# Attention sums turned and multiplied with Wo one slot later, in a two-part kernel on one core

## The chip, the core and the metric

The kernel runs on one core of a Trainium2 chip. The time is the device time of one launch in microseconds: 4896.63 us as the median of three runs (4894.68 to 4904.67). The engines named below are PE (TensorE: matrix products and transposes; its weight loads are listed apart as PEld), DVE (VectorE), ACT (ScalarE), POOL (GpSimd) and SP (SyncE, which issues the transfers). All data is float32.

## The reference

The input x is 8 sequences of 512 tokens of 128 features. Two parts follow one another, each behind a layer norm and with its input added to its output:

```python
x = x + attn(layernorm(x), Wqkv, Wo)     # 16 heads of 8, causal; weights 1/(lam - s),
                                         # lam by 4 Newton steps, then normalized
x = x + stack(layernorm(x), ...)         # 6 layers:
for i in range(6):
    x = attn_layer(shift_tokens(x), Wqkv[i], q_scale[i], k_scale[i], Wo[i]) + x
    x = ffn_layer(shift_tokens(x), ln_g[i], ln_b[i], W1[i], b1[i], W2[i], b2[i]) + x
```

attn_layer has 16 heads of 64, normalizes and rotates queries and keys, and lets each window of 32 tokens see itself and the window before. The softmax weights multiply the values, the sum is divided by the sum of the weights, and the heads' outputs are multiplied with Wo (1024 to 128). ffn_layer is a layer norm, a product to 2 x 341 features, a gated Gelu and a product back to 128. shift_tokens moves half of the features one token on.

## The kernel before

The first part is a generator, `stieltjes`, that yields four times in each of its four Newton steps (16 yields, `STEPS`, to a batch of four heads). Sequence 1 runs beside sequence 0 in a stage of its own before the second part begins. The other sequences of the first part are then advanced a few steps per slot of the second part, until `goal` reaches their total some 150 slots before the end. What the second part needs is forced earlier by `need`, which calls `enter` (a fetch of `x2`, a layer norm and four transposes into `xT[b]`). Reads of x and x2 go through `fetch`, into the tile `xb`: for the projection of a sequence, for its end (`sequence_end`, which adds the result to x and writes `x2`), and for `enter` (the last layer's own read of x2 into `xr` aside).

The second part is one loop over slots, t. A unit is a pair of layer and sequence (48 units). The sequences go in groups, (0, 1), then (2, 3, 4), then (5, 6, 7), and within a group the layers are the outer order, so a sequence's next layer comes two units later in the first group and three units later in the others. A unit has four quarters of two pairs of heads, so eight pairs and eight slots. In slot t the code has, in this order:

- `turn(a)`: queries and keys of pair t are transposed (L665) and copied by ACT (L670).
- `gather(last)`: for pair t - 3, 64 small products of weights and values (L719) into the PSUM tile `po2`; DVE takes the reciprocal of the weights' sums (L727) and multiplies (L728) into the SBUF tile `o2`, here called `o`.
- `turn_weights(done)`: the weights of pair t - 2 are transposed (L708) and copied by ACT (L709).
- `prepare_qk`: half of the queries and keys of a coming quarter. Two products (L599, each in two matmuls) and, for each, a square on ACT (L605), the rotation on DVE (L608), a sum on DVE (L614) and an addition on POOL (L616), and at the end the scaling on POOL (L627).
- `exponentials` of pair t - 1 on ACT (L701), and `gelus`.
- `turn_sums(last)`: `o` is transposed (L736, four transposes) and copied by ACT into `oT` (L740).
- `weigh(a)`: 64 small products for the scores of pair t (L684) into the PSUM tile `s2`, then the mask on DVE (L689), the maximum (L694) and the subtraction on POOL (L695).
- `prepare_v`: the values of the coming quarter (L636, ACT copy L639), and every other slot `spread`, 18 transfers of values on SP's queue, and in some slots the loads of the next layer's weights.
- some pieces of the feed-forwards that wait in `parts`.
- `leave(last)`: `oT` times Wo (L744), summed in the PSUM tile `acc` over a unit's eight pairs. After the eighth, DVE adds `acc` to `xT[b]` (L924) and the feed-forward is put into `parts`.

The feed-forward is a generator with seven pieces (eight in the last layer): shift (POOL, L567 to L569); transposes, copy and statistics (L765, L767, L771, L772); normalization (L775 to L778); transposes and ACT's scaling (L785, L787); the product for the gates and its bias (L793, L796); Gelu and the second product and its multiplication with the gates (L754, L804, L807); the product back and the addition to `xT[b]` (L814, L817). One piece is run in each slot, but four in each slot in which the pair that leaves belongs to the first group. There the same sequence's next layer is opened (`open_quarter`, whose shift reads `xT[b]`) three slots after the slot of L924, so a unit's feed-forward must have been traced by then.

PSUM is divided among four pools: two banks for the first part, three with the tag "mm" that rotate among the second part's tiles, one pair of banks with the tag "two" and a single buffer, which `po2` and `s2` use in turn, and one bank for `acc`:

```python
both = ps_b.tile([P, 2, N], F32, name="s2", tag="two")     # weigh
po = ps_b.tile([P, 2, N], F32, name="po2", tag="two")      # gather
```

The order of the code is a priority, not the order of issue: the framework orders each engine's instructions at build time by readiness in an estimate of its own, and puts in the waits. What an engine has been given it runs in that order.

Of the kernel before, what the change touches and what calls it, by code (L numbers as in the profile page):

```python
# [9 lines left out]
F32 = mybir.dt.float32  # L10
# [6 lines left out]
P = 128  # L17
N = 512
NT = N // P
D = 128  # L20
# [9 lines left out]
DHL = 64  # L30
# [20 lines left out]
def tile_kernel(  # L51
# [36 lines left out]
    groups_of = ((0, 1), (2, 3, 4), (5, 6, 7)) if NB == 8 else (tuple(range(NB)),)  # L88
    units = [(l, b) for grp in groups_of for l in range(DEPTH) for b in grp]
# [5 lines left out]
    pj = ctx.enter_context(tc.tile_pool(name="pj", bufs=1))  # L95
# [71 lines left out]
    def streams(pools, bank1):  # L167

        ns_p, dp, tr, pj, sm = pools

        def fetch(src):
            xb = pj.tile([P, NT, D], F32, name="xb", bufs=2)
            nc.sync.dma_start(xb, src.rearrange("(c p) d -> p c d", p=P))
            return xb

# [333 lines left out]
    tp = ctx.enter_context(tc.tile_pool(name="tp", bufs=1))  # L509
# [36 lines left out]
    def load_wo(l, hv):  # L546
        wo = wp.tile([P, NPAIR // 2, D], F32, name="wo", tag=f"wo{hv}")
        nc.sync.dma_start(wo, f_wo[l][hv * HC : (hv + 1) * HC, :].rearrange("(c p) d -> p c d", p=P))
        return wo

    def load_tables(l, h):
        tab = wp.tile([P, 2, 4, DHL], F32, name="tab", tag=f"tab{h}")
        nc.sync.dma_start(tab, tabs[l][:, 2 * h : 2 * h + 2])
        return tab
# [19 lines left out]
    def bank(shape, name):  # L574
        if done_steps >= (4 * NB + 1) * STEPS:
            turns["n"] += 1
            if turns["n"] % 5 > 2:
                return ps_1.tile(shape, F32, name=name, tag="p1")
        return ps_a.tile(shape, F32, name=name, tag="mm")

    PQ = 2
# [77 lines left out]
    def turn(a):  # L659
        g, p = a["g"], a["p"]  # L660
        a["qT"] = qT = []
        for t in range(2):
            pt = bank([P, N], "ptq")
            for c in range(NT):
                nc.tensor.transpose(  # L665
                    pt[:, c * P : (c + 1) * P],
                    g["qn"][:, c, t, 2 * p : 2 * p + 2, :].rearrange("p h e -> p (h e)"), ident,
                )
            q = tp.tile([P, N], F32, name=f"qT{t}")
            nc.scalar.copy(q, pt)  # L670
            qT.append(q)
# [27 lines left out]
    def exponentials(a):  # L699
        flat = a["pr"].rearrange("p c e k -> p (c e k)")  # L700
        follow(nc.scalar.activation(flat, flat, AF.Exp), marks["act"])  # L701

    def turn_weights(a):
        pr = a["pr"]
        a["prT"] = prT = tp.tile([P, NT, P], F32, name="prT")
        pT = bank([P, NT, P], "pT2")
        for c in range(NT):
            nc.tensor.transpose(pT[:, c, :], pr[:, c].rearrange("p e k -> p (e k)"), ident)  # L708
        nc.scalar.copy(prT, pT)  # L709

    def gather(a):
        g, p, prT = a["g"], a["p"], a["prT"]
        po = ps_b.tile([P, 2, N], F32, name="po2", tag="two")
        po = po[:, :, 0 : NT * (DHL + 1)].rearrange("p e (c f) -> p e c f", c=NT)
        for n in range(NQ):
            c, u = n // UB, n % UB
            for e in range(2):
                rows = slice(e * KB, (e + 1) * KB)
                nc.tensor.matmul(  # L719
                    po[u * QB : (u + 1) * QB, e, c, :],  # L720
                    lhsT=prT[rows, c, u * QB : (u + 1) * QB],
                    rhs=g["v3"][rows, n, p, :],
                    start=True, stop=True,
                )
        a["o"] = o = tp.tile([P, NT, 2, DHL], F32, name="o2")
        rs = tp.tile([P, 2, NT], F32, name="rs", bufs=2)
        nc.vector.reciprocal(rs, po[:, :, :, DHL])  # L727
        nc.vector.tensor_tensor(  # L728
            o.rearrange("p c e f -> p e c f"), po[:, :, :, 0:DHL],
            rs.unsqueeze(3).to_broadcast([P, 2, NT, DHL]), ALU.mult,  # L730
        )

    def turn_sums(a):
        pt = bank([P, N], "po3")
        for c in range(NT):
            nc.tensor.transpose(  # L736
                pt[:, c * P : (c + 1) * P], a["o"][:, c].rearrange("p e f -> p (e f)"), ident
            )
        a["oT"] = oT = tp.tile([P, N], F32, name="oT2")
        nc.scalar.copy(oT, pt)  # L740

    def leave(a, wo, acc):
        pp = a["g"]["qt"] * PQ + a["p"]
        nc.tensor.matmul(  # L744
            acc, lhsT=wo[:, pp % (NPAIR // 2), :], rhs=a["oT"],
            start=(pp == 0), stop=(pp == NPAIR - 1),
        )
# [3 lines left out]
    def gelus():  # L751
        if waiting:
            flat = waiting.pop().rearrange("p k n -> p (k n)")
            g = follow(nc.scalar.activation(flat, flat, AF.Gelu), marks["act"])  # L754
            marks["act"] = follow(
                nc.scalar.preload_act_table_set("natural_log_exp_and_others"), g
            )
# [74 lines left out]
    LAG = 2  # L832
# [4 lines left out]
    wo = {hv: load_wo(l0, hv) for hv in range(2)}  # L837
# [5 lines left out]
    def need(b):  # L843
        if b not in entered:
            advance(ready_at.get(b, 0))
            enter(b)
            entered.add(b)

    def open_quarter(i):
        u, qt = quarters[i]  # L850
        groups.append(begin(u, qt, shifted(units[u][1], ep) if qt == 0 else groups[-1]["xs"]))

    def prepared(g):
        u, qt = g["u"], g["qt"]
        spread(g)
        if u + 1 < len(units) and units[u + 1][0] != units[u][0]:
            if qt % 2:
                wq[qt // 2] = load_qkv(units[u + 1][0], qt // 2)
# [8 lines left out]
    pairs, parts, acc = [], [], None  # L867
    slots = len(quarters) * PQ
    t = -1
    while t < slots + LAG + 1 or parts:  # L870
        i, p = t // PQ, t % PQ
        a = done = last = ahead = None
        if 0 <= i < len(quarters):
            a = dict(g=groups[i], p=p)
            pairs.append(a)
        if LAG <= t < len(pairs) + LAG:
            done = pairs[t - LAG]
        if LAG + 1 <= t < len(pairs) + LAG + 1:
            last = pairs[t - LAG - 1]
        if a:  # L880
            turn(a)
        if last:
            gather(last)
        if done:
            turn_weights(done)

        i, h = (t + 1) // PQ + 1, (t + 1) % PQ
        if i < len(quarters):
            if h == 0:
                open_quarter(i)  # L890
            ahead = groups[i]
            cs = (2 * h, 2 * h + 1)
            prepare_qk(ahead, wq[ahead["qt"] // 2], tab[h], cs)
            u = ahead["u"] + 1
            if ahead["qt"] == NS // PQ - 1 and u < len(units) and units[u][0] != units[u - 1][0]:
                tab[h] = load_tables(units[u][0], h)
        if 1 <= t < len(pairs) + (0 if a else 1):
            exponentials(pairs[t - 1])
        gelus()
        if last:  # L900
            turn_sums(last)
        if a:
            weigh(a)
        if ahead:
            prepare_v(ahead, wq[ahead["qt"] // 2], cs)
            if h == PQ - 1:
                prepared(ahead)
        many = 1
        if last and len(parts) + 1 and units[last["g"]["u"]][1] in groups_of[0] and len(groups_of) > 1:
            many = 4  # L910
        for _ in range(many):
            parts = [n for n in parts if next(n, n) is not n]
        if last:
            u, qt = last["g"]["u"], last["g"]["qt"]
            l, b = units[u]
            hv = qt // 2
            if last["p"] == 0 and qt == 0:
                acc = ps_c.tile([P, N], F32, name="acc")
            leave(last, wo[hv], acc)
            if last["p"] == PQ - 1:  # L920
                if qt % 2 and u + 1 < len(units) and units[u + 1][0] != l:
                    wo[hv] = load_wo(units[u + 1][0], hv)
                if qt == NS // PQ - 1:
                    nc.vector.tensor_tensor(xT[b], xT[b], acc, ALU.add)  # L924
                    parts.append(feed_forward(u, *w12[0]))
        t += 1
        u = (t + 6) // NS
        if u < len(units):
            need(units[u][1])
        lead = 3 * NS * DEPTH  # L930
        goal = 5 * STEPS + (total - 5 * STEPS) * (t + 1) // (slots - lead - NS)
        advance(min(goal, total))
# [51 lines left out]
```

## Time and profile before

| | |
|---|---|
| median of three runs | 4896.63 us |
| the profiled execution's own time | 4896.56 us |
| its span | 4894.9 us |
| PE busy | 4172.2 us, 85% |
| DVE busy | 4155.8 us, 85% |
| ACT busy | 3517.7 us, 72% |
| POOL busy | 2990.9 us, 61% |
| L740, ACT's copy of the turned sums | 384 of 585 ns, 283.8 us idle before them |
| L744, the products with Wo | 768 of 606 ns |
| L728, the division on DVE | 384 of 684 ns |

A line of a group gives the source line, the engine, the operation, what it writes and reads, the count, the busy time and the mean of one, and after the bar the idle time of that engine just before these instructions with the work that ended it. A line of a wait gives the total, the times and the longest, in microseconds. Idle time of an engine that is not the bottleneck costs nothing. The first part ends near 3520 us, and it is thin from about 3430 us on; after that the second part is alone.

### The profile page before, as it was taken

The numbers are of one execution on the slowest core, as the hardware profiler recorded it, in microseconds if no ns is written. First come the engines' busy times: TensorE is split into PE (matmuls) and PEld (weight loads), VectorE is DVE, ScalarE is ACT, GpSimd is POOL, SyncE is SP. The second block draws the span as 40 slices with busy tenths as digits, with TensorE's granted clock in tenths as the row PEclk, the third lists the DMA queues.
The fourth block names the chain that finished last, engine by engine and source line by source line (L and its number), as shares of the span: only waits on it lengthen the run. The fifth ranks groups of instructions, "written<-read, shape, count | busy, mean of one in ns | idle before, by whom it ended". The sixth has DMA issues, their size and how long they took to land. (4 is left out here: it accounts for less than half of the span.)

```text
span 4894.9 us, 165932 instructions
## 1 busy us (share of the span) xinstructions
PE 4172.2 (85%) x68749; PEld 2525.4 (52%) x68749; DVE 4155.8 (85%) x9460; ACT 3517.7 (72%) x6298; POOL 2990.9 (61%) x3822
## 2 busy tenths in 40 slices
PE   4555788888888888898888888888999999999998
PEld 1232455544555454554555555555566666666664
DVE  8787888988999989988889999898787777777775
ACT  6898777777777777766777777777566666666664
POOL 3543666656566655666666665666566666666763
PEclk7666899999999999999999999999999999999999
DMA  1000222222222222222222222222233333333332
GB/s 47 1 1 26 52 65 52 62 59 54 59 54 69 61 56 46 65 59 46 63 53 57 53 48 67 47 55 59 65 89 79 80 87 71 85 73 83 85 72 57
DMA packets 558914, 288.89 MB, mean 59 GB/s; under 512 B 97580, under 2 KB 541264, under 8 KB 558160
## 3 DMA queue, kind: packets, MB, share of 16 engines
q1 hardware_dynamic: 558160, 278.26, 24.4%
q8 instruction: 543, 8.90, 0.8%
q14 instruction: 211, 1.73, 0.1%
HBM read 66.21 MB, written 7.34 MB: 15 GB/s over the span
## 5 line engine op out<-in xcount | busy, mean ns | idle before, releaser
L616 POOL TENSOR_TENSOR qn<-qr 128x512 f32<-128x512 f32 x768 | 979.1, 1275 | 1157.1 <-DVE qr L608 1128.4
L608 DVE TENSOR_TENSOR qr<-m,tab 128x1024 f32<-128x1024 f32 x768 | 935.6, 1218 | 293.8 <-ACT sq L605 245.9
L627 POOL TENSOR_TENSOR qn<-qn,ss 128x512 f32<-128x512 f32 x768 | 785.5, 1043 | 113.5 <-ACT ss L624 91.4
L599 PE MATMUL m<-wqkv,xs 128*128 128x512 f32 x1536 | 767.4, 616 | 54.9 <-ACT qT L670 43.8
L281 ACT ACTIVATE d<-ns,lam 128x416 f32<-128x416 f32 (+7 forms) x1024 | 577.8, 623 | 138.4 <-DVE lam L299 103.2
L605 ACT ACTIVATE sq<-m 128x512 f32<-128x512 f32 x768 | 459.1, 598 | 261.9 <-DVE ss L614 180.6
L264 POOL TENSOR_TENSOR df<-ns,lam 128x160 f32<-128x160 f32 (+7 forms) x1024 | 400.6, 427 | 330.5 <-DVE lam L299 207.7
L284 DVE BATCH_NORM_STATS2 stw<-d 128x6 f32<-128x416 f32 (+7 forms) x1024 | 520.5, 561 | 95.7 <-ACT d L282 94.5
L670 ACT COPY qT<-ptq 128x512 f32<-128x512 f32 x768 | 426.4, 586 | 167.2 <-PE ptq L665 165.2
L614 DVE TENSOR_REDUCE ss<-sq 128x8 f32<-128x512 f32 x768 | 517.5, 674 | 0.0
L636 PE MATMUL pv<-wqkv,xs 128*128 128x256 f32 x1536 | 450.1, 416 | 58.4 <-DVE qr L608 43.7
L665 PEld LDWEIGHTS ptq<-ident,qn 128*128 128x128 f32 x3072 | 356.1, 143 | 255.7 <-issue 91.4
L665 PE MATMUL ptq<-ident,qn 128*128 128x128 f32 x3072 | 454.6, 282 | 38.7 <-ACT v L639 22.1
L695 POOL TENSOR_TENSOR pr<-pr,nm 128x512 f32<-128x512 f32 x384 | 400.2, 1042 | 68.7 <-DVE nm L694 57.0
L316 PE MATMUL dTp<-ident,ns 128*128 128x128 f32 x1280 | 245.4, 314 | 224.1 <-ACT ns L304 134.2
L740 ACT COPY oT<-po 128x512 f32<-128x512 f32 x384 | 224.5, 585 | 283.8 <-PE po L736 283.5
L252 PE MATMUL s<-kn,qj 32*32 32x224 f32 (+15 forms) x4096 | 365.7, 430 | 71.3 <-DVE mn L256 59.0
L744 PE MATMUL acc<-oT,wo 128*128 128x512 f32 x768 | 402.2, 606 | 2.7 <-ACT oT L740 2.7
L719 PE MATMUL po<-v,prT 64*32 64x65 f32 x24576 | 393.7, 226 | 6.8 <-DVE pr L689 6.6
L599 PEld LDWEIGHTS m<-wqkv,xs 128*128 128x128 f32 x1536 | 265.4, 197 | 255.2 <-issue 121.3
L282 ACT ACTIVATE d<-d 128x1856 f32<-128x1856 f32 (+1 forms) x256 | 393.0, 1535 | 0.0
L719 PEld LDWEIGHTS po<-v,prT 64*32 64x32 f32 x24576 | 289.8, 106 | 167.4 <-issue 107.2
(135 smaller groups left out, 8118.3 us busy)
## 6 DMA issues: line engine op xcount, KB each, us to landing
v<-v SPq DMA_DIRECT2D x2304, 65.0 KB
v<-v SPq DMA_DIRECT2D x768, 48.8 KB
wqkv<-in_L_ffn_Wqkv_dram SPq DMA_DIRECT2D x72, 256.0 KB
v<-v SPq DMA_DIRECT2D x384, 32.5 KB
wqkv<-in_L_ffn_Wqkv_dram SPq DMA_DIRECT2D x72, 128.0 KB
wo<-in_L_ffn_Wo_dram SPq DMA_DIRECT2D x36, 256.0 KB
tab<-tabs SPq DMA_DIRECT2D x36, 256.0 KB
w<-in_L_ffn_W_dram SPq DMA_DIRECT2D x18, 341.0 KB
```

What stands on the lines that cost most here:

```text
L281: nc.scalar.activation(o, n, AF.Ln, bias=lam[:, c : c + 1])
L284: nc.vector.bn_stats(t["st"][:, 4 * rb + a].rearrange("p u k -> p (u k)"), o)
L599: nc.tensor.matmul(m.rearrange("p t h e -> p t (h e)"), lhsT=xs[:, c * P : (c + 1) * P], rhs=wqkv[:, 0:2, q0 : q0 + HQ * DHL], start=True, ...
L605: marks["act"] = nc.scalar.activation(sq, m.rearrange("p t h e -> p (t h) e"), AF.Square)
L608: nc.vector.tensor_tensor(qr, m.unsqueeze(1).to_broadcast([P, 2, 2, HQ, DHL]), tab[:, i].rearrange("p (k t) e -> p k t e", k=2).unsqueeze( ...
L614: nc.vector.tensor_reduce(ss[:, i, :], sq, axis=AX.X, op=ALU.add)
L616: nc.gpsimd.tensor_tensor(g["qn"][:, c].rearrange("p t h (u e) -> p (t h) u e", u=2), halves_of[:, 0], halves_of[:, 1, :, ::-1, :], ALU.add,)
L627: nc.gpsimd.tensor_tensor(qc, qc, ss[:, i, :].unsqueeze(2).to_broadcast([P, 2 * HQ, DHL]), ALU.mult)
L636: nc.tensor.matmul(pv[:, i], lhsT=xs[:, c * P : (c + 1) * P], rhs=cols, start=True, stop=True,)
L665: nc.tensor.transpose(pt[:, c * P : (c + 1) * P], g["qn"][:, c, t, 2 * p : 2 * p + 2, :].rearrange("p h e -> p (h e)"), ident,)
L670: nc.scalar.copy(q, pt)
L719: nc.tensor.matmul(po[u * QB : (u + 1) * QB, e, c, :], lhsT=prT[rows, c, u * QB : (u + 1) * QB], rhs=g["v3"][rows, n, p, :], start=True, s ...
```

## The change

The pair whose sums are turned, copied and multiplied with Wo is no longer the pair that is gathered in the same slot (`last`, t - 3) but the one gathered a slot before (`gone`, t - 4). The tile `o2` gets a second buffer, and `xb` gives one of its two up. The loop runs one slot more. Everything that hangs on the product with Wo comes a slot later: the addition to `xT[b]`, the reload of Wo and the start of the feed-forward. In the first group the feed-forward's pieces per slot go from four to nine, so that all of them are traced in the slot after it is put into `parts`.

```diff
         def fetch(src):
-            xb = pj.tile([P, NT, D], F32, name="xb", bufs=2)
+            xb = pj.tile([P, NT, D], F32, name="xb")
...
-        a["o"] = o = tp.tile([P, NT, 2, DHL], F32, name="o2")
+        a["o"] = o = tp.tile([P, NT, 2, DHL], F32, name="o2", bufs=2)
...
-    while t < slots + LAG + 1 or parts:
+    while t < slots + LAG + 2 or parts:
...
+        if LAG + 2 <= t < len(pairs) + LAG + 2:
+            gone = pairs[t - LAG - 2]
...
-        if last:
-            turn_sums(last)
+        if gone:
+            turn_sums(gone)
...
-        if last and len(parts) + 1 and units[last["g"]["u"]][1] in groups_of[0] and len(groups_of) > 1:
-            many = 4
+        if gone and len(parts) + 1 and units[gone["g"]["u"]][1] in groups_of[0] and len(groups_of) > 1:
+            many = 9
         for _ in range(many):
             parts = [n for n in parts if next(n, n) is not n]
-        if last:
-            u, qt = last["g"]["u"], last["g"]["qt"]
+        if gone:
+            u, qt = gone["g"]["u"], gone["g"]["qt"]
             l, b = units[u]
             hv = qt // 2
-            if last["p"] == 0 and qt == 0:
+            if gone["p"] == 0 and qt == 0:
                 acc = ps_c.tile([P, N], F32, name="acc")
-            leave(last, wo[hv], acc)
-            if last["p"] == PQ - 1:
+            leave(gone, wo[hv], acc)
+            if gone["p"] == PQ - 1:
```

More of the change, by code (lines that the diff above doesn't have):

```diff
@@ L869, in tile_kernel @@
     t = -1
-    while t < slots + LAG + 1 or parts:
+    while t < slots + LAG + 2 or parts:
         i, p = t // PQ, t % PQ
-        a = done = last = ahead = None
+        a = done = last = gone = ahead = None
         if 0 <= i < len(quarters):
```

## The prediction

> **What bounds the kernel now.** I read the page first (shares of the span in 40 slices), then three long stretches of the span, the groups of instructions by line, the waits stretch by stretch, and the timeline around one ordinary slot and one unit boundary. The slices first:
>
> ```profile
> span 4894.9 us, 165932 instructions
> ...
> PE   4555788888888888898888888888999999999998
> ...
> DVE  8787888988999989988889999898787777777775
> ```
>
> There are four stages. Up to about 555 us the first part runs alone. Then both parts run together until about 3430 us, and from there the second part alone. In the stretches below the columns are length, then busy time of PE, PE's weight load, DVE, ACT and POOL:
>
> ```profile
> 555.00:1790.00 1235.00, 1068.53 (x17300) 632.78 (x17277) 1108.02 (x2589) 917.95 (x1644) 763.66 (x994) 0.96 0.25 59
> 1790.00:3430.00 1640.00, 1416.43 (x23038) 845.30 (x23038) 1469.27 (x3430) 1244.08 (x2225) 1032.08 (x1352) 0.96 0.24 55
> 3430.00:4895.00 1465.00, 1396.80 (x25730) 896.00 (x25730) 1135.07 (x1916) 906.02 (x1772) 944.99 (x929) 0.99 0.34 77
> ```
>
> The reader is to see that the first two have DVE at 90% and PE at 86%, neither full, and that the last one is PE's, at 95% with its drain and 97% without (389.15 of 400 us between 3800 and 4200). So a PE wait that goes in the last stage is worth its full length, and one that goes in the first two only part of it. The two groups that the change is about, the turning of the divided sums (L736) and the scores of the next pair (L684), with idle time and its releasers at the end of the line:
>
> ```profile
> L736 PE MATMUL po<-ident,o 128*128 128x128 f32 x1536 | 244.1, 281 | 82.9 <-DVE o L728 50.9 <-ACT prT L709 20.0 <-DVE sw L294 3.8
> L684 PE MATMUL s<-qT,qT 64*32 64x64 f32 x24576 | 348.8, 227 | 6.7 <-DVE o L728 4.5 <-DVE lam L270 1.3 <-ACT qT L670 0.9
> ```
>
> PE stands 50.9 us in all before the turning, because the division on DVE (L728) is late. The scores hardly wait for it, but only because they come right behind the turning: the sums (`po2`) and the scores (`s2`) share one PSUM tile with the tag "two" and one buffer, so L684 too may not start before L728 has read `po2`. An ordinary slot of the last stage shows the order:
>
> ```profile
> 4199.93 0.69 DVE L728 TENSOR_TENSOR o<-po,rs 128x512 f32<-128x512 f32 x1
> 4199.99 1.88 PE L599 MATMUL m<-wqkv,xs 128*128 128x512 f32 x4
> ...
> 4201.71 0.60 PE L736 MATMUL po<-ident,o 128*128 128x128 f32 x4
> ...
> 4202.24 0.86 PE L684 MATMUL s<-qT,qT 64*32 64x64 f32 x64
> ```
>
> Here the division ends at 4200.62, under the four projections, and PE runs without a gap. The turning takes 0.53 us of PE (4201.71 to 4202.24). The waits by stretch (total, times, longest), first for 600 to 1800 us, then 1800 to 3400, then 3450 to 4840:
>
> ```profile
> PE pn L785 <- DVE xt L778: 20.1, 10, 5.1
> ...
> PE po L736 <- DVE o L728: 8.8, 10, 2.6
> ```
> ```profile
> PE po L736 <- DVE o L728: 24.4, 14, 4.1
> ```
> ```profile
> PE po L736 <- DVE o L728: 11.4, 22, 3.2
> ```
>
> The remaining 6.3 us, six times, lie in the drain and between these stretches.
>
> **The change, part by part.** No instruction is added or dropped; 1536 transposes, 384 copies and 768 products with Wo move one slot later. All sums are against the profiled execution, 4896.56 us (span 4894.9 and 1.7 around it); the median of the runs shown, 4896.63, is the same within 0.1.
>
> *The turning no longer waits.* In the next slot its input is ready, so the 50.9 us at L736 go. What is late next is L684, which stands 0.53 us further back and needs the same division. So of each wait at most 0.53 us is saved: 10 x 0.53 = 5.3 in the first stretch, 14 x 0.53 = 7.4 in the second, about 8 of the 11.4 in the last (22 waits of 0.52 mean, some longer than 0.53), 6 x 0.53 = 3 in the rest. In the first two stretches DVE is the busier engine and I count half, 6.4; the others count whole. Sum: -17 us. Its bounds: nothing, if the order of issue puts the turning where it covers nothing; 51 if the division is never late for the scores. I take 17, since the shared tile is plain in the code and the 4.5 us at L684 show that this wait exists. The 20.0 us before L736 that ACT's copy at L709 ends are for the PSUM bank, not for the sums, and stay.
>
> The trace says of the first two stretches that DVE is busiest, at 90%, and the change takes no work from it. [...] I keep the half, because PE's lateness also starves DVE there (13.6 us of idle time at L689 behind the scores of L684 in the second stretch).
>
> *Copy and product.* ACT's copies (384 of 0.585 us) and PE's products (768 of 0.606) have the same neighbours one slot on. The copy waits for PE 283.5 us in all, but ACT is 62 to 76% busy and what is queued behind it, the second square (L605), mostly waits for DVE anyway (L614, 180.6 us). I count 0; if that cover is gone, one 0.6 us copy in each of the 52 bad slots is 31 us, half of it 16, in either direction.
>
> *One buffer for `xb` instead of two.* Its users are the fetches of x and x2. A fetch for the next stage reads what the write of `x2` has just stored, so it waits for that write in any case, and the other users are some ten slots apart. I count 0. If each of the 16 fetches of x (one for the projection and one for the end of each of eight sequences) had to wait for one landing (2.36 us for x<-xb in the chain of waits), 38 us.
>
> *Queues.* SP's loads of Wo (36 of 256 KB) come a slot later and so does their first reader. The `v` spreads keep their places. POOL's shifting copies for the feed-forward (L567, L569: 1.2 us) come one slot later with it. Nothing here sets the end: 0, or 1.2 us for each of 48 units, 58, if POOL's own chain were the bound; it is 61 to 65% busy.
>
> *The feed-forward of the first group (slots 0 to 95).* This is the price. There two sequences alternate, so a unit's feed-forward must be traced before the same sequence's next layer is opened. Before, it had two passes of up to 4 pieces, four (to the normalized, turned input) in one slot and three in the next. It now starts a slot later and must be through at the same point: `many = 9` runs all seven in one slot. One boundary now:
>
> ```profile
> 1096.43 1.24 PE L785 MATMUL pn<-ident,xt 128*128 128x128 f32 x4 [5.08 <-DVE xt L778]
> ...
> 1104.55 1.02 PE L793 MATMUL gp<-xn_ffn,w 128*128 128x512 f32 x2
> ...
> 1113.90 2.85 PE L814 MATMUL y<-gate,w 128*128 128x512 f32 x6
> ...
> 1118.24 0.61 POOL L569 COPY xs<-xT 64x511 f32<-64x511 f32 x1
> ...
> 1121.82 1.88 PE L599 MATMUL m<-wqkv,xs 128*128 128x512 f32 x4
> ```
>
> Between L785 and L793 lies a slot of other PE work (1097.47 to 1104.34), under which ACT's L787 is done. That cover goes. Bare, this step costs what the very end of the program shows, where nothing covers it:
>
> ```profile
> 4875.64 1.25 PE pn L785 x4
> 4876.92 0.79 ACT xn_ffn L787
> 4877.75 5.47 PE gp L793 x6
> ```
>
> that is 0.86 us from the end of L785 (4876.89) to L793. And every further link (gate, Gelu with its two table loads, product, y) then runs while DVE still has that slot's work. I price it by its nearest row, the wait before L785, which exists where four pieces are in one slot: 20.1 / 10 = 2.0 us, while in the second stretch, with one piece a slot, L785 waits 0.0 us in 15 units. Eleven units (0 to 10) pay 0.86 + 2.0 = 2.9: +31 us. Bounds: nothing, since m at L599 now starts 2.97 us after its input is there (1118.85 to 1121.82) and the next slot's turning and sums can fill PE; or the longest wait, 5.1 + 0.86 each, 66 us. I take 31, the mean row.
>
> *The end.* One more pass; the last unit's chain (division, turning, copy, product, feed-forward) has the same links, the one before it is a slot later in an almost empty stretch: +1, between -3 (waits in the drain) and +3.
>
> Sum: 4896.6 - 17 + 31 + 1 = 4911.6, say 4912.
>
> **The rivals.** *Faster:* the joined feed-forward is covered, so its term is nothing. 4896.6 - 17 + 1 = 4881; with the full 51 and no loss 4847. For it speaks the slack of 2.97 us before m, and that Gelu, product and y already share a slot with only 7.2 us of PE wait (8 times) before y. Against it the 20.1 us. It decides by more than 0.2% (10 us, about what a measurement of this kernel can tell from no change) as long as a unit pays under 0.5 us (16 - 10 = 6 over 11). *No change:* a unit pays 0.5 to 2.4 us, or the wait moves to the scores in full and the pieces are covered: 4897. *Much slower:* each of the eleven pays the longest wait: 4896.6 - 17 + 66 + 1 = 4947. For it: in a slot with seven pieces each of DVE's five rounds for the feed-forward queues behind that slot's own DVE work at 90% load.
>
> **How the numbers follow.** Forecast (slower by 10 to 35 us) 0.36; much slower 0.16; faster 0.29; no change 0.19. So faster 0.29, same 0.19, slower 0.52. The framework sets each engine's order at build time (ACT runs the copy L740 between two squares that the code has ahead of it), so each moved instruction can shift others; I widen for that. The range leaves out a tenth on each side: from 4872, past most of the faster case, to 4950, past the much slower one's value. The forecast's own range is 4906 to 4932.
>
> **What would show it.** Right: the wait of L736 for L728 near 0; L684 waiting for L728 25 to 35 us instead of 4.5; PE waits before L785 to L814 in 600 to 1800 us up by some 30 us and that stage some 25 us longer; the last stage 8 us shorter. Wrong: no new wait at L684 (then the shared tile doesn't matter, and it is faster by up to 50), or no new wait in the feed-forward of the first group.

## The result

The changed kernel takes 4910.15 us (median of ten runs, 4906.24 to 4915.07), the kernel before beside it 4894.68 us (ten runs, 4886.42 to 4904.67). The ratio is 1.0032 with a 95% interval of 1.0023 to 1.0042: slower by 0.32%, some 15.5 us. The profiled execution of after took 4906.97 us, 10.4 us more than the profiled one of before.

### The profile page after: what moved, and what is told of

It is laid out like the page before. It is cut to its first block, busy times and chain, and to the rows that moved or that the text cites. A ratio compares the mean times of both kernels' runs of the same rounds, so it can differ in the third digit from the quotient of the medians.

```text
span 4905.3 us, 165599 instructions
## 1 busy us (share of the span) xinstructions
PE 4180.4 (85%) x68749; PEld 2528.7 (52%) x68749; DVE 4143.5 (84%) x9460; ACT 3518.4 (72%) x6298; POOL 2990.6 (61%) x3822
## 3 DMA queue, kind: packets, MB, share of 16 engines
q1 hardware_dynamic: 558160, 278.26, 24.3%
## 5 line engine op out<-in xcount | busy, mean ns | idle before, releaser
L670 ACT COPY qT<-ptq 128x512 f32<-128x512 f32 x768 | 427.1, 588 | 161.1 <-PE ptq L665 156.5
L636 PE MATMUL pv<-wqkv,xs 128*128 128x256 f32 x1536 | 449.7, 414 | 77.7 <-DVE qr L608 57.3
L665 PEld LDWEIGHTS ptq<-ident,qn 128*128 128x128 f32 x3072 | 347.0, 141 | 264.2 <-issue 126.2
L665 PE MATMUL ptq<-ident,qn 128*128 128x128 f32 x3072 | 441.3, 279 | 44.2 <-ACT v L639 26.6
L252 PE MATMUL s<-kn,qj 32*32 32x224 f32 (+15 forms) x4096 | 354.7, 423 | 63.0 <-DVE mn L256 55.0
L740 ACT COPY oT<-po 128x512 f32<-128x512 f32 x384 | 224.7, 585 | 222.0 <-PE po L736 221.6
```

Of the source, the lines that this page charges most:

```text
L636: nc.tensor.matmul(pv[:, i], lhsT=xs[:, c * P : (c + 1) * P], rhs=cols, start=True, stop=True,)
L665: nc.tensor.transpose(pt[:, c * P : (c + 1) * P], g["qn"][:, c, t, 2 * p : 2 * p + 2, :].rearrange("p h e -> p (h e)"), ident,)
```

## The profile after

The page of the changed kernel, its 40 slices:

```profile
span 4905.3 us, 165599 instructions
...
PE   4565788888888888899888888898999999999998
...
DVE  8787888988888888889898899898787787777776
```

The same stretches as before (length, then busy time of PE, its weight load, DVE, ACT and POOL, the granted clock, the share of the DMA engines and GB/s):

```profile
555.00:1790.00 1235.00, 1065.67 (x16892) 629.41 (x16896) 1084.58 (x2542) 909.45 (x1623) 746.27 (x977) 0.93 0.25 58
1790.00:3430.00 1640.00, 1415.13 (x22980) 838.30 (x22973) 1465.07 (x3398) 1240.94 (x2212) 1030.48 (x1350) 0.95 0.24 55
3430.00:4905.00 1475.00, 1411.64 (x26131) 910.33 (x26128) 1148.65 (x1995) 915.13 (x1802) 958.98 (x942) 0.99 0.34 78
```

The first of them is where the kernel changed: in the same 1235 us it gets through less of everything. DVE falls from 1108.02 to 1084.58 us of work and POOL from 763.66 to 746.27. PE's busy time hardly falls, although it runs 408 matmuls fewer; its granted clock went from 0.96 to 0.93. The two groups of the turning and the scores:

```profile
L736 PE MATMUL po<-ident,o 128*128 128x128 f32 x1536 | 239.9, 278 | 16.2 <-ACT prT L709 15.4 <-DVE qr L608 0.5
...
L684 PE MATMUL s<-qT,qT 64*32 64x64 f32 x24576 | 350.7, 226 | 23.6 <-DVE o L728 22.4 <-DVE sw L298 0.8
```

The turning's 50.9 us of waits for the division are gone, and the scores wait 22.4 us for it instead of 4.5. So 33 of 55.4 us of this wait disappeared, and the kernel is slower all the same. To see where the time came in, I followed the second ACT copy (L670) of each slot through both traces and took the difference, after minus before:

| from slot to slot | before, us | after, us | difference, us |
|---|---|---|---|
| 3 to 67 | 839.8 | 834.7 | -5.1 |
| 67 to 99 | 426.0 | 451.6 | +25.6 |
| 99 to 383 | 3019.3 | 3013.1 | -6.2 |
| before slot 3 and after slot 383 together | 609.8 | 605.9 | -3.9 |

Single profiled executions scatter by up to some 10 us at such marks (e7 below, whose first group has its pieces as before, takes 10.0 us more from slot 3 to 67), so only the large figure is worth reading: the loss lies in the first group (slots 0 to 95), and against before it shows in the group's last third. The stretch of both kernels by engine (before first, then after):

```profile
1400.20:1826.20 426.00, 363.97 (x5889) 215.57 (x5880) 381.99 (x892) 324.74 (x577) 273.29 (x364) 0.96 0.26 61
```
```profile
1391.30:1842.90 451.60, 382.45 (x5906) 223.70 (x5907) 387.40 (x908) 326.99 (x581) 272.39 (x364) 0.91 0.25 58
```

The work is the same within a few instructions. PE is busy 18 us longer with it at a lower clock, and DVE's idle time rises from 44.0 to 64.2 us. One unit boundary of after shows what a joined feed-forward looks like (start, duration, and in brackets the idle time before it with what ended it):

```profile
1092.13 0.48 PE L785 MATMUL pn<-ident,xt 128*128 128x128 f32 x1 [0.63 <-DVE xt L778]
...
1094.88 0.78 ACT L787 ACTIVATE xn_ffn<-pn,vec 128x512 f32<-128x512 f32 x1 [3.35 <-PE pn L785]
1095.68 1.28 ACT L754 ACT_TABLE_LOAD   x1
...
1095.71 5.18 PE L793 MATMUL gp<-xn_ffn,w 128*128 128x512 f32 x6
...
1097.83 0.75 DVE L796 TENSOR_SCALAR gate<-gp,vec 128x512 f32<-128x512 f32 x1 [1.01 <-PE gp L793]
...
1099.54 0.75 DVE L796 TENSOR_SCALAR gate<-gp,vec 128x512 f32<-128x512 f32 x1 [0.84 <-PE gp L793]
...
1101.72 1.48 ACT L754 ACTIVATE gate<-gate 128x1536 f32<-128x1536 f32 x1 [4.75 <-DVE gate L796]
```

PE has hardly any idle time here after L785. What has changed is that the six products for the gates follow straight on a thin stretch and take 5.18 us. DVE then stands before each of the three biases, and ACT, which already has Gelu and its table load at the head of its queue, stands 4.75 us. Summed over the eleven boundaries between 555 and 1790 us, in the waits (total, times, longest) of before and then of after:

```profile
PE pn L785 <- DVE xt L778: 20.1, 10, 5.1
...
ACT gate L754 <- DVE gate L796: 0.6, 3, 0.2
```
```profile
DVE gate L796 <- PE gp L793: 24.9, 27, 1.6
...
ACT gate L754 <- DVE gate L796: 21.1, 8, 5.1
...
PE pn L785 <- DVE xt L778: 16.7, 16, 4.1
...
PE gp L793 <- ACT xn_ffn L787: 6.3, 8, 0.9
```

The same stretch with L793's own instructions alone (busy time of PE and of its weight load), before and after:

```profile
555.00:1790.00 1235.00, 33.29 (x66) 10.50 (x66) 0.96 0.25 59
```
```profile
555.00:1790.00 1235.00, 53.45 (x66) 17.63 (x66) 0.93 0.25 58
```

So the joined feed-forward brought three things: gate products at a lower clock (+20 us of PE), DVE waiting for them (+25), and ACT waiting behind its own Gelu (+20). The experiments ask which part of the change costs the time, and which of these three it is.

## The experiments

The theory: the price is the joined feed-forward of the first group, and the late turning of the other groups gains a little. The rivals: the price is the single `xb`; the price is the late turning itself, by the order that it forces; among the causes inside the join, the lower clock, DVE's throughput, or ACT's standing. Each run is compared with the kernel before on the same chip.

| run | ratio to before | 95% interval | median, us |
|---|---|---|---|
| e1_xb1: before, `xb` with one buffer | 1.0015 | 1.0007 to 1.0023 | 4899.05 |
| e2_join: before, feed-forward joined (nine pieces) | 1.0036 | 1.0024 to 1.0048 | 4908.65 |
| e5_join5: before, five pieces | 1.0004 | 0.9993 to 1.0015 | 4893.82 |
| e6_join6: before, six pieces | 1.0047 | 1.0035 to 1.0059 | 4915.84 |
| e3_split: after, first group as before | 1.0000 | 0.9991 to 1.0008 | 4891.44 |
| e4_split_xb2: as e3, two `xb`, one `o2`, turning ahead of gathering | 1.0137 | 1.0121 to 1.0154 | 4960.29 |
| e8_masks: before, two masks in bfloat16 | 0.9993 | 0.9983 to 1.0002 | 4885.62 |
| e7_split_xb2: as e3, two `xb`, masks as in e8 | 1.0001 | 0.9993 to 1.0010 | 4893.78 |
| e9_fill: after, PE kept busy ahead of L785 | 1.0039 | 1.0026 to 1.0051 | 4910.98 |
| e10_bias_act: before, gate bias on ACT | 1.0046 | 1.0032 to 1.0059 | 4915.52 |
| e11_after_bias_act: after, gate bias on ACT | 1.0017 | 1.0008 to 1.0026 | 4899.00 |
| e12_unjoin: after, feed-forward spread over two slots | 0.9989 | 0.9980 to 0.9998 | 4890.35 |

### One buffer for `xb`, alone

```diff
-            xb = pj.tile([P, NT, D], F32, name="xb", bufs=2)
+            xb = pj.tile([P, NT, D], F32, name="xb")
```

> The kernel before with one buffer for xb and nothing else. Theory 1 (the forecast: the joined feed-forward pieces of the first group cost about 31 us, the later turning saves about 17, xb is free): 4895 us, within 5 of before. Theory 2 (the joined pieces are free and the single xb buffer is what costs, because the fetches and the layer norms behind them move to other places): 4908 to 4918 us. Theory 3 (the time follows the order that the framework happens to give, whatever is changed): some 10 us off in either direction, with no stage that stands out.

It costs 0.15%, some 7 us, where I had counted nothing. That is a little over the 5 us of theory 1 and well under the 13 or more of theory 2. No wait of the trace names it. The first products behind a fetch and layer norm (L202) wait 8.3 us for ACT, 7.8 in before. In after they wait 24.3, and that can therefore not be put down to `xb` alone. The groups of after and of this run, by line:

```profile
L202 PE MATMUL pq<-xnT,wT 128*128 128x512 f32 x16 | 12.5, 876 | 24.3 <-ACT xnT L195 24.3
```
```profile
L202 PE MATMUL pq<-xnT,wT 128*128 128x512 f32 x16 | 12.5, 873 | 8.4 <-ACT xnT L195 8.3
```

### The join, alone

```diff
-            many = 4
+            many = 9
```

> The kernel before with nine pieces of the feed-forward per slot in the first group instead of four, so that all seven are traced in one slot; the sums are turned where they were. Theory 1: 4895 + 31 = 4926 us, all of it lost between 555 and 1790 us, with new waits of PE before L793 and more at half clock. Theory 2: 4895 us. Theory 3: as for e1_xb1.

Without the late turning the join costs 0.36%, 17.6 us, as much as the whole change and little over half of what theory 1 had. Its waits between 555 and 1790 us are like those of after, with a longer one before L785:

```profile
PE pn L785 <- DVE xt L778: 25.6, 9, 5.2
...
ACT gate L754 <- DVE gate L796: 20.8, 7, 5.1
...
DVE gate L796 <- PE gp L793: 19.1, 19, 3.4
```

Its time is not lost where after loses it, however: by the same marks this profile takes 6.3 us more than before from slot 3 to 67, 3.4 us from 67 to 99 and 3.6 us from 99 to 383. So the totals of the two agree, but the 25.6 us of after in the last third are not what the join alone does.

### The late turning without the join

The pairs of the first group leave in the slot in which they are gathered, as in the kernel before, with four pieces a slot. Those of the other groups leave a slot later, as in after, and `xb` has one buffer.

```diff
+    def early(a):
+        return units[a["g"]["u"]][1] in groups_of[0]
...
-        if LAG + 2 <= t < len(pairs) + LAG + 2:
+        if LAG + 2 <= t < len(pairs) + LAG + 2 and not early(pairs[t - LAG - 2]):
             gone = pairs[t - LAG - 2]
+        if last and early(last):
+            gone = last
...
-            many = 9
+            many = 4
```

> The changed kernel with the pairs of the first group turned, copied and multiplied in the slot in which they are gathered, four pieces per slot there, as before; the pairs of the other two groups a slot later, as changed; one buffer for xb. Theory 1: the price of the first group goes, the saving in the later stages stays (4 in the second stretch, 8 in the last, 3 in the drain): about 4882 us. Theory 2: xb still costs 15 to 20: 4895 to 4903 us.

1.0000. So the whole price of the change, 0.32%, goes with what it does to the first group. The saving that theory 1 added to that (4882 us) does not appear beside before. Against e1, which has the same single `xb`, the late turning of the other two groups is 0.15%, 7 us, faster.

### Five and six pieces

`many = 5` lets the gate products (L793) into the slot of the transposes, `many = 6` also Gelu and the second product.

> The kernel before with five pieces of the feed-forward per slot in the first group instead of four: the normalized input's transposes (L785), ACT's scaling (L787) and the product for the gates (L793) are then in one slot, and Gelu, the second product and the product back in the next. Joining all seven cost 0.36%, and there PE spent 46 us instead of 33 on L793 in the first group, at a lower granted clock. Theory 1a (the price is paid where L793 follows straight on the stall before L785, as half-clock time): most of the 0.36%, 0.25 to 0.4%, and L793 near 46 us. Theory 1b (the price is the length of the whole chain in one slot, Gelu and the last products too): under 0.15%.

> As e5_join5 with six pieces in the first slot, so that only the product back (L814) is left for the next. Theory 1a: as e5_join5, 0.25 to 0.4%. Theory 1b: between e5_join5 and the 0.36% of all seven, rising with the number of pieces.

Five pieces cost nothing that can be measured, six cost 0.47%, where either theory had 0.4% at most, and no less than all seven (0.36%). The fifth piece moves the gate products, and with it come the lower clock (L793 46.12 us of PE, 33.29 in before) and DVE's wait for them. L793 alone between 555 and 1790 us, and the waits there, of five pieces:

```profile
555.00:1790.00 1235.00, 46.12 (x66) 16.16 (x66) 0.95 0.25 59
```
```profile
DVE gate L796 <- PE gp L793: 20.5, 21, 3.4
```

and of six:

```profile
DVE gate L796 <- PE gp L793: 20.7, 20, 3.4
...
ACT gate L754 <- DVE gate L796: 14.6, 8, 4.2
```

The gate products' slowness (L793 takes 47.24 us in e6) and DVE's wait are in both. Only the costly one has Gelu waiting on ACT, since Gelu with its table load is put into ACT's queue in the same slot as the gates it needs. So neither the first nor the second of the three costs anything that can be seen by itself, at the size that they have in e5, and the third is a candidate. The sixth piece brings the second product (L804) and its multiplication into the slot as well, so it is not the only one.

### Two buffers for `xb`, and where the turning stands

In e4 `xb` has its two buffers again and `o2` has one, and the late pair is turned ahead of the next gathering, which writes that buffer again.

```diff
-            xb = pj.tile([P, NT, D], F32, name="xb")
+            xb = pj.tile([P, NT, D], F32, name="xb", bufs=2)
...
-        a["o"] = o = tp.tile([P, NT, 2, DHL], F32, name="o2", bufs=2)
+        a["o"] = o = tp.tile([P, NT, 2, DHL], F32, name="o2")
...
+        if gone and gone is not last:
+            turn_sums(gone)
         if last:
...
-        if gone:
+        if gone and gone is last:
             turn_sums(gone)
```

> As e3_split, but with two buffers for xb and one for o2, which needs the turning of the pair gathered a slot before to be traced ahead of the gathering of the next pair. Theory 1: as e3_split, 4882 us, less or more by what the place of the turning changes. Theory 2: 12 to 15 us below before, 4882 us, and faster than e3_split by 15 to 20.

1.37% slower, where both theories had 4882 us, and nearly all of it in the last stage, where PE is the bound (slot 228 to 383: +62.5 us against before). The waits from 3600 to 4700 us:

```profile
PE ptq L665 <- ACT v L639: 28.6, 75, 0.9
...
PE s L684 <- DVE o L728: 13.5, 15, 1.0
```

The scores now wait for the division in a stage in which after has no such wait at all, and the turning of the queries (L665) waits 28.6 us for a copy that it waited 0.2 us for in after, between the same times. The likely reason is that what the four transposes covered in their old place is uncovered. These two name 42 of the 62 us. To give `xb` its second buffer and leave the order alone, two masks were made smaller, in a control by themselves and then with e3:

```diff
-    far = k1.tile([P, N], F32, name="far")
+    far = k1.tile([P, N], BF16, name="far")
...
-    band = k2.tile([P, NT, KB], F32, name="band")
+    band = k2.tile([P, NT, KB], BF16, name="band")
```

> The kernel before with the tables far and band in bfloat16 and nothing else, the control to e7_split_xb2. No instruction more or less; L689 (0.679 us) and L256 read one bfloat16 operand. Within 0.1% of before, if the type of a mask does not change what these instructions take.

> The late turning in the second and third group only, as in e3_split (level with before, 0.0%), with two buffers for xb and two for o2; the room comes from the two mask tables, far and band, in bfloat16 (their values, 0 and very large numbers, need no more). If the single xb buffer costs the 0.15% that it cost alone, and the late turning of two groups saves what e3_split showed beside it: 0.15% faster than before, about 7 us. If the effect of xb is only the order that happens to come out: within 0.1% of before.

The masks alone are worth nothing that can be measured (0.9993, the interval reaches 1.0002). With them, two buffers for `xb` and two for `o2`, the late turning of two groups gives 1.0001. That is no better than e3 with one `xb` buffer, so the 7 us of e1 do not add up with the rest. And the control to e7 is e8, which has the same masks: beside it, on the same chip, the late turning of two groups is slower, by 4 us by the ratios to before (whose intervals overlap) and by 8 us by the medians. Beside e1 it was 7 us faster. So a gain of the late turning is not shown, and whether the 0.15% of e1 is the price of the single buffer or of the order that came out with it stays open too.

### The clock

Four products of 128 by 512 whose result nobody reads are put ahead of L785 in the feed-forwards of the first group. They are extra work that is meant to keep PE's clock up.

```diff
+        if b in groups_of[0]:
+            fill = bank([P, N], "fill")
+            for _ in range(4):
+                nc.tensor.matmul(fill, lhsT=ident, rhs=far, start=True, stop=True)
         pn = bank([P, N], "pn")
```

> The changed kernel with four more products (128x512, about 0.43 us each, into a bank that nobody reads) ahead of L785 in the feed-forwards of the first group, so that PE works where it stood before L785. In the changed kernel DVE stands 24.9 us before L796 for L793 between 555 and 1790 us, against nothing before, and L793 takes 53 us there instead of 33. Theory A1 (L793 is late because it runs at half clock behind the stall): L793 near 35 us, the wait before L796 under 10 us, and the time 10 us or more below the changed kernel, at most 0.15% over before. Theory A2 (L793 is late because the chain through ACT's scaling has no other slot's work over it, at any clock): the wait before L796 stays near 25 us, and the time stays at +0.3% or rises by up to 19 us.

They did what they were meant to: the granted clock of the stage is back at 0.96, and the gate products (four lines further down here, L797) take 38.16 us instead of 53.45. The stage as a whole, and then those products alone:

```profile
555.00:1790.00 1235.00, 1083.04 (x17001) 637.66 (x17002) 1089.30 (x2549) 913.12 (x1626) 747.13 (x978) 0.96 0.25 58
```
```profile
555.00:1790.00 1235.00, 38.16 (x66) 13.62 (x66) 0.96 0.25 58
```

DVE's wait for the gates halves too (11.7 us; 24.9 in after), but ACT's before Gelu stays:

```profile
ACT gate L754 <- DVE gate L800: 16.1, 8, 4.1
...
DVE gate L800 <- PE gp L797: 11.7, 14, 1.9
```

and so does the time, 1.0039. So the gate products and DVE's wait went about as theory A1 had it, and the time as A2 had it. POOL gets through 747.13 us of work in this stretch, as in after (746.27) and not as in before (763.66). So the lower clock looks like a companion of the join and not its price. This run alone does not prove it, since the filler's own time (PE is 17 us busier) may hide part of a gain; e5, with the gate products at 46.12 us and no price that can be measured, says the same without a filler.

### DVE's load

The bias of the gates is moved from DVE to ACT, in the kernel before and in the changed one.

```diff
-            nc.vector.tensor_scalar(
-                gate[:cn, k], gp[:cn], vec[:cn, 3 + NCH + k, l : l + 1], None, ALU.add
+            nc.scalar.activation(
+                gate[:cn, k], gp[:cn], AF.Identity, bias=vec[:cn, 3 + NCH + k, l : l + 1]
             )
```

> The kernel before with the bias of the gates (L796, three of 0.74 us in each of 48 units on DVE) added by ACT instead (Identity with a bias, as L787, 0.79 us each). Theory A (where both parts run, DVE at 90% is what sets the time): the 27 units there give up 27 x 2.2 = 60 us of DVE, and 20 to 60 us of it show in the time, 0.4 to 1.2% faster. Theory B (the order and PE's waits set it, DVE is no bound): within 0.2% of before, or slower, since ACT gets 2.4 us per unit more.

> The changed kernel with the bias of the gates on ACT, to be set against e10_bias_act, as after against before. Theory A (what the change costs is DVE standing before L796): that wait moves to ACT, which is 74% busy there, and the difference shrinks from 15.5 us to under 8. Theory B (the cost is the length of the joined chain, whichever engine waits): the difference stays at 12 us or more.

In the two mixed stages 78 of these 0.74 us instructions (54.6 us in before) leave DVE, and the kernel before becomes 0.46% slower. Its two mixed stages:

```profile
555.00:1790.00 1235.00, 1064.78 (x17155) 632.79 (x17152) 1089.12 (x2548) 938.93 (x1675) 762.34 (x993) 0.95 0.25 59
1790.00:3430.00 1640.00, 1404.26 (x22884) 839.96 (x22884) 1441.24 (x3353) 1263.53 (x2259) 1020.18 (x1340) 0.96 0.24 55
```

DVE has less to do in each of them (1108.02 and 1469.27 in before) and nothing goes faster for it. The lag comes in the second stage: this run is level with before at slot 99 (-0.2 us) and 16.5 us behind at slot 240. With the change, the same edit does the opposite, which neither theory had: it is 15.0 us behind before at slot 99, as far as after is (16.7), and has won nearly all of it back at slot 240 (0.9 behind; after 14.8). So with the bias on ACT the changed kernel is 0.3% faster than the unchanged one, 4899.00 against 4915.52. The lag at the end of the first group is there with the bias on either engine; with the bias on ACT, ACT waits for the gate products itself, between 555 and 1790 us of e11:

```profile
ACT gate L796 <- PE gp L793: 29.1, 28, 2.2
```

What the second stage makes of an edit that looks the same in both kernels differs by some 30 us, and I could name no wait for that.

### The join taken apart

In the first group the product with Wo, the addition (L924) and the start of the feed-forward are put ahead of the slot's pieces. So the feed-forward has two slots again, as before the change: three pieces in the slot of the addition and up to five in the next.

```diff
-        many = 1
-        if gone and len(parts) + 1 and units[gone["g"]["u"]][1] in groups_of[0] and len(groups_of) > 1:
-            many = 9
-        for _ in range(many):
-            parts = [n for n in parts if next(n, n) is not n]
-        if gone:
...
+        soon = gone and units[gone["g"]["u"]][1] in groups_of[0] and len(groups_of) > 1
+        fresh = False
+
+        for turn_of in (0, 1):
+            if turn_of == (0 if soon else 1) and gone:
...
+                        parts.append(feed_forward(u, *w12[0]))
+                        fresh = True
+            if turn_of == 0:
+                many = 1
+                if soon:
+                    many = 3 if fresh else 5
+                for _ in range(many):
+                    parts = [n for n in parts if next(n, n) is not n]
```

> The changed kernel with all its late turning and its one buffer for xb, but in the first group the product with Wo and the addition to xT are traced ahead of the feed-forward's pieces, so that the pieces start in the slot of the addition and are divided among two slots, three and then the rest. In the changed kernel a unit of the first group has one slot of 29.9 us and one of 12.5 where before had 18.4 and 19.8 (time between the copies L670 of successive slots, mean over units), and its other six slots are 2.2 us shorter in all. Theory A (the joining is the whole price of the change): the long slot goes; if the other six keep their 2.2 us a unit, 24 us, the time is about 4870 us, 0.5% below before; if they lose it again, about level with before, 4895 us. Theory B (starting in the slot of the addition only moves the stall from L785 to L765, which then stands for POOL's shift): no gain on the changed kernel, 4905 us or more. Theory C (any other order than that of before costs some 0.1 to 0.4%, whatever it does): 4900 to 4915 us.

0.9989 (0.9980 to 0.9998): the whole price is gone, about as theory A had it without a lasting gain in the other six slots, and the kernel is 0.11% faster than before and, by the ratios, 0.43% (21 us) faster than after. It is the fastest form of this change that was run, though its lead over before is only as large as other edits moved by chance. Its span, its two groups, and between 555 and 1790 us its waits and L793 alone:

```profile
span 4886.9 us, 165573 instructions
```
```profile
L684 PE MATMUL s<-qT,qT 64*32 64x64 f32 x24576 | 350.0, 225 | 24.3 <-DVE o L728 22.4 <-DVE sw L298 0.8 <-issue 0.7
...
L736 PE MATMUL po<-ident,o 128*128 128x128 f32 x1536 | 239.3, 278 | 10.1 <-ACT prT L709 9.7
```
```profile
PE px L765 <- POOL xs L569: 29.0, 10, 8.4
...
PE gp L793 <- ACT xn_ffn L787: 4.5, 7, 1.0
...
ACT gate L754 <- DVE gate L796: 1.9, 4, 0.8
```
```profile
555.00:1790.00 1235.00, 31.50 (x66) 10.69 (x66) 0.95 0.25 59
```

The shorter waits of the late turning are kept as in after (no wait at L736 for the division, 22.4 us at L684). L793 takes 31.50 us again and Gelu waits 1.9. And PE now stands 29.0 us before the feed-forward's first transposes, behind POOL's shift, a wait longer than any that the join brought to PE. The stage is not longer for it. By the marks of the slots this kernel takes 12.8 us less than before from slot 3 to 67 and 10.3 us more from 67 to 99. So a part of what after loses in the last third is there without the join, and against this kernel, its nearest neighbour, after loses 7.7 us up to slot 67 and 15.3 us in the last third.

## Why the prediction was right, and where not

The forecast was 4912 us, slower with a chance of 0.52; it is 4910.15. The direction and the cause's place are right. Two of its terms were too large in opposite directions, and one mechanism was wrong, so that the sum came so close is luck.

**The turning no longer waits (-17): mechanism right, size too large.** The waits behaved as forecast: L736 from 50.9 to 0, L684 from 4.5 to 22.4 us where 25 to 35 were expected. That is 33 us of waiting saved, more than the 24 that the sum counted. But waiting saved is not time saved. From slot 99 to 383 after is 6.2 us shorter. The term that failed most plainly is "about 8 of the 11.4 in the last": the lag behind before shrinks there by some 3 us only (15.1 us at slot 232, 12.3 at slot 376), and from slot 264 to 376 a unit takes 69.15 us in before and 69.22 in after. The reason is in the waits of the last stage, of before from 3450 to 4840 us and of after from 3450 to 4850:

```profile
PE pv L636 <- DVE qr L608: 12.1, 20, 1.3
```
```profile
PE pv L636 <- DVE qr L608: 19.2, 21, 1.1
...
PE ptq L665 <- ACT v L639: 4.3, 3, 3.7
```

L665 had no such line in before. As much as the turning no longer waits for comes back at other products: 7.1 us more at L636, behind DVE, and 4.3 us at L665, behind ACT. The forecast asked what is late next and stopped at the first answer, L684, which does not wait for the division in this stage. What the late turning of two groups is worth lies, by e3 against e1 and e7 against e8, between 7 us gained and 8 us lost.

**The conversion by a half.** In the first two stretches I counted half, because DVE was the busier engine. The row said that DVE was at 90%. e10 took 54.6 us of work off DVE and was 0.46% slower, while the same edit made the changed kernel faster (e11). So DVE's load did not set the time there. What did set it, and so the half, no run shows; I take it to be the order of issue.

**Copy and product, queues (0 each): held.** The copy (L740) waits less for PE than before (97.1 to 68.3 us from 1800 to 3400), and e3, which moves all of these in two groups, is at 1.0000.

**One `xb` (0): not settled.** Alone it measured 0.15%, about 7 us of the 38 that were its bound. Beside the late turning, a second buffer brought nothing (e7 against e3).

**The joined feed-forward (+31): place right, size half, mechanism wrong.** The loss lies in the first group, as forecast: slots 3 to 99 take 20.5 us more in the profiles, where "some 25 us" was written, e2 puts the join at 17.6 us, and e3 and e12 show that it is the whole price. Its price per unit is 1.6 us instead of 2.9. The step that failed is "I price it by its nearest row, the wait before L785". That wait did not grow in after, it fell from 20.1 to 16.7; with the join alone (e2) it rose by 5.5 us, not by 31. The bare link of 0.86 us to L793 is there (6.3 us in eight of the boundaries). PE's waits before L785, L793 and L814 together went from 28.5 to 29.9 us (36.1 in e2), where 30 more were forecast. Nor is the price seen to be paid eleven times alike: in after slots 3 to 67 lose nothing against before and slots 67 to 99 lose 25.6 us, while e6 loses 15.4 and 9.2.

**What the price consists of stays open.** It is hardly the lower clock (e9, and e5 with most of it at no cost), nor DVE's wait for the gates (e5 has it at no cost), nor PE's waits by their sum (e12 has more of them and is the fastest). ACT standing before Gelu goes with the slow kernels: 14.6 to 21.1 us in e2, e6, e9 and after, 1.9 us or less in before, e1, e3, e5, e8 and e12, whose ratios lie between 0.9989 and 1.0015. (e4 and e10 are slow without it, but they lose their time behind the first group.) With the bias on ACT (e11), ACT stands 29.1 us before L796 instead, and slot 99 is late as well. But this is a correlation, and a loose one: in after, 14.8 of the 21.1 us fall ahead of 1420 us, where no time is lost against before, and only 6.3 lie in the slow third. It was not isolated by a run of its own.

**The end (+1): held.** From the last slot's copy to the end it is 49.4 us in before and 49.3 in after.

The one term that the runs show is the join, at 18 against 15.5 measured for the whole; `xb` lies between nothing and 7 us, and the sign of the late turning is not known. The sum of the forecast, +15, agrees with the measurement because +31 was nearly twice what the join takes and -17 at least twice what the late turning saves, and the two errors cancelled.

## What to carry to other kernels

Waits that go or come at one engine are not microseconds of the span, least of all when no engine of a stage is at its limit: PE lost 33 us of waiting here and gained little, even in the last stage (some 3 us), and in e12 it took on 29 us of new waiting at no loss. A chain over four engines that starts a slot later but must be through at the same point is better begun earlier within its slot than pressed into one, which was worth 0.43% here (e12 against after). Edits that take no work away (a buffer, an operation on another engine) moved this kernel by 0.15 to 0.46% with no wait to account for it, so a gain of that size needs a control with the same edit and without the idea, and has to be read against that control: e7 looks level beside before and slower beside e8.

## What the runs showed of the hardware

The clock fell where PE had stood for 2.35 us at most. At the boundary shown above, PE's granted clock by stretches around it (the third number from the right):

```profile
1085.00:1089.00 4.00, 2.75 (x73) 1.73 (x71) 3.65 (x11) 2.99 (x7) 1.35 (x2) 1.00 0.37 83
1089.00:1092.00 3.00, 1.41 (x64) 1.17 (x64) 3.00 (x11) 0.94 (x4) 2.33 (x3) 0.70 0.51 115
1092.00:1095.70 3.70, 2.54 (x7) 1.23 (x7) 3.35 (x7) 0.80 (x2) 1.98 (x2) 0.50 0.40 107
1095.70:1098.00 2.30, 2.30 (x4) 1.18 (x4) 1.21 (x5) 1.26 (x1) 0.00 (x0) 0.50 1.04 319
1098.00:1101.00 3.00, 3.00 (x5) 1.06 (x4) 1.70 (x6) 0.00 (x0) 0.00 (x0) 0.59 0.03 8
1101.00:1105.00 4.00, 3.35 (x29) 1.63 (x31) 3.07 (x10) 3.25 (x3) 1.98 (x5) 1.00 0.00 0
```

The clock is at 0.50 from 1092 to 1098 us; with the parts of the rows beside them (0.70 and 0.59 over 3 us each) that makes about 1090.2 to 1100.5 us, some 10 us, an estimate that takes the clock in those rows as either 1.00 or 0.50. The longest idle time of PE just before is 2.35 us, ahead of the 64 small products that start at 1090.10; the other gaps are 0.5 to 0.6 us. So six gate products that follow a thin stretch pay for it: 5.18 us for six here, 53.45 instead of 33.29 us over the stage. The six products of L804 right behind them, most of whose time lies in the row at 1.00, take 2.74 us. PE has no gap from 1094.12 us on, so by the same estimate the lower clock lasted some 6 us into full work here.

The other surprise is how little that mattered: four idle-filling products brought the clock of the stage back from 0.93 to 0.96, and the time stayed where it was (1.0039, after 1.0032), with the filler's own time in it.
